# A graph attention kernel: products of half blocks in the first projection too, another order of products, and other first and last graphs

## The chip, the cores and the metric

The kernel runs on one core of one Trainium2 chip. The metric is the device time of one execution in microseconds. TensorE (PE in the profile) multiplies and transposes into eight banks of PSUM; VectorE (DVE) and ScalarE (ACT) do the element-wise work and read the banks; SyncE (SP) issues the DMAs; GpSimd (POOL) has one small power operation per graph. Each engine works through its own queue in order, and semaphores make one wait for another.

## What is computed

Thirty-two graphs of 512 nodes with 512 features go through a normalization, two layers of graph attention and a residual addition. All arithmetic is in float32.

```python
def gat_layer(x, mask, W, a_src, a_dst, bias, concat):
    xl = (x @ W).reshape(B, N, H, F)
    asrc = jnp.einsum('bnhf,hf->bnh', xl, a_src)
    adst = jnp.einsum('bnhf,hf->bnh', xl, a_dst)
    e = jax.nn.leaky_relu(asrc[:, :, None, :] + adst[:, None, :, :], 0.2)
    e = jnp.where(mask[..., None], e, NEG_INF)
    attn = jax.nn.softmax(e, axis=1)
    out = jnp.einsum('bsdh,bshf->bdhf', attn, xl)
    ...
    return out + bias

h = jnp.maximum(_layernorm(x, axis=-1), 0.0)
h = jax.nn.elu(gat_layer(h, mask, W1, att_src1, att_dst1, b1, concat=True))
x = x + gat_layer(h, mask, W2, att_src2, att_dst2, b2, concat=False)
```

The first layer has four heads of 256 features (W1 is 512x1024), the second has one head of 512 (W2 is 1024x512). The mask is the adjacency with its diagonal set.

## The kernel before

Nodes and features lie on 128 partitions in blocks of 128: four node blocks, four blocks of input features, eight of hidden features.

**One graph.** `load` and `load_adj` bring x and the adjacency (two `adj` buffers, so that the third and fourth tile wait until `masks` has used the first two). `norm` is a generator of five steps: statistics, then for each node block the normalized rows and four transposes (`pht`, L187), which ScalarE copies with a Relu into `ht` (one buffer). `masks` makes the 0 / big mask in bfloat16 (three buffers, each used until the second layer of its graph is done, three graphs on); `turned_masks` transposes it (`pm`, L208).

`project1` (L306) multiplies `ht` by W1. For two heads at a time and each node block it makes two results of 128x258 in a PSUM bank, each of four multiplications over the input features; ScalarE copies each into `xl` (L317). The columns 0 and 1 of each head are the score weights, which `weights1` reduces from W1 and the attention vectors, so that the scores come out of the same product. In float32 a multiplication is two instructions of the profile, which is why 64 multiplications show as 128.

`Soft` is the attention. `columns(i)` picks the scores out of `xl`; `rows(i)` transposes them (`pas`, L227), copies them (`ras`, L229) and sends them through DRAM (two DMAs on SP: `das`, L231, and `oas`, L233), so that every partition has the source scores as a row. `first(h)` makes the normalizers of one head: for each node block a Prelu (L263), a masked minimum (L266, VectorE) and an exponential with its sum (L270), then a logarithm and the small rows `r` (L276, L277). `turn(h)` spreads `r` as `rows` does (`prr` on TensorE, `rrr`, `drr`, `orr`). `second(h)` makes the attention weights `p` (L292 on VectorE, L296 on ScalarE, L300 on VectorE).

`gather1` (L325) multiplies `xl` by `p`, two blocks of features per head, eight steps in all, with the elu (ScalarE L339 into `e`, VectorE L340 and L341 into `h1`). `project2` (L371) is the second projection. It is cut into halves of rows, features and columns, and instead of eight products of half blocks it makes seven, of sums of blocks (the Strassen-Winograd form). `sums2` (L355) makes four sums of `h1` on VectorE, `weights2` four sums of W2. A product is four multiplications; three banks per row block m ("a", "g", "b") take the products, and a bank is read between two products that accumulate into it: products 1, 5, 6 and 4 are copied by ScalarE, 2, 7 and 3 are added to `xl2` by VectorE (L404). `gather2` (L429) multiplies the second layer's `p` by `xl2` in four steps, and VectorE adds the residual `xr` (L441), to which `residual_bias` has added the bias (L427); the sum goes out.

**The order.** All is unrolled. Tile's planner orders the instructions of VectorE, ScalarE, GpSimd and SP by its own estimates of when they can run, with the program's order as priority; TensorE's order is written out by hand (`manual_schedule`). Round i of the main loop has three stretches on TensorE: `project1` of graph i + 1; four steps of `gather2` of graph i - 1 and fourteen products of `project2` of graph i; eight steps of `gather1` of graph i + 1. The transposes of other steps are put between them: `late.turn(0)` (second layer of graph i - 1) after the first step of `project1`, `s1.rows(0)` after its fifth of eight; `s1.rows(1)` after the first step of `gather2`, `s1.turn(0)` after the third, the other heads' between the products of `project2`; the second layer's `rows` behind the third step of `gather1`. PSUM has six banks for products (tag "mm") and two for transposes (tag "tp").

Ahead of the loop stand `load`, `weights1`, `norm`, `masks` and `weights2` for graph 0; round -1 has only graph 0's first layer, with all four heads turned before its `gather1`. In the last full round two steps of `gather2` come before and two after `project2`, and the second layer of the last graph follows alone.

## Time and profile before

| | |
|---|---|
| Median of three runs | 3241.77 us (3239.64 to 3250.65) |
| Profiled execution | 3244.41 us, of which the span of its instructions is 3242.4 us |
| Mean granted clock of TensorE | 0.988 |
| DMA read and written | 232.53 MB and 34.54 MB, 82 GB/s over the span |

```profile
## 4 chain that ended last, share of the span: by engine, by line
PE 64%; DMA 13%; DVE 12%; ACT 10%; issue 1%; SPq 0%; POOL 0%; ACTq 0%; DVEq 0%
...
L313 PE MATMUL pxl<-w_sb,ht 128*128 128x258 f32 x4096 | 935.3, 385 | 3.1 <-DVE j L111 3.1
L333 PE MATMUL po<-p,xl 128*128 128x512 f32 x2048 | 890.2, 594 | 0.0
```

The first two lines are the chain of work that ended last, by engine. The others are groups of instructions: line, engine, operation, tiles, shapes and count; then the busy time, the mean length of one in ns, and the idle time ahead of them with what ended it. The mean of one is longer than its share of the busy time, as the multiplications overlap: 935.3 us by 4096 is 0.23 us each. In rows of a timeline the first two columns are start and length in us, and the bracket at the end is the engine's idle time before the row and what ended it. In rows of stretches, after the stretch and its length, stand the busy times with the instructions counted, then the granted clock (1.00 is full speed) and the DMAs' share and GB/s.

### The profile page before, as it was taken

How to read it: one execution, taken by the hardware profiler on the slowest of the kernel's cores; microseconds unless marked ns; L12 is line 12 of the kernel's file. 1: busy time of each engine (PE TensorE's matmuls, PEld its weight loads, DVE VectorE, ACT ScalarE, POOL GpSimd, SP SyncE). 2: the span in 40 equal slices, each digit the busy share in tenths (PEclk: the TensorE clock that was granted, in tenths of full speed). 3: DMA queues.
4: the chain of work that ended last, by engine and by line, in shares of the span. 5: the costliest groups of instructions: out<-in, count | busy, mean ns of one | idle time of the engine just before them, and what ended most of it. 6: DMA issues, size and time to landing. Idle time of an engine off the chain costs nothing.

```text
span 3242.4 us, 35403 instructions
## 1 busy us (share of the span) xinstructions
PE 3142.2 (97%) x12032; PEld 2125.1 (66%) x12032; DVE 2282.4 (70%) x5163; ACT 1785.5 (55%) x3873; POOL 33.2 (1%) x38
## 2 busy tenths in 40 slices
PE   5899999999999999999999999999999999999987
PEld 4576676666676666776666776666766766766754
DVE  7677766677766777766777766777766777766672
ACT  3555655556555556555556555556555555555561
POOL 0000000000000000000000000000000000000000
PEclk8899999999999999999999999999999999999998
DMA  5122222222322122322122322222322222321121
GB/s 185 43 66 82 95 98 76 65 86 81 101 92 82 60 88 84 101 91 76 62 88 88 98 89 80 65 82 95 98 85 72 75 82 95 98 77 60 63 69 49
DMA packets 121462, 269.38 MB, mean 83 GB/s; under 512 B 15552, under 2 KB 22592, under 8 KB 121280
## 3 DMA queue, kind: packets, MB, share of 16 engines
q1 hardware_dynamic: 121280, 267.12, 25.5%
q8 instruction: 94, 1.54, 0.2%
q14 instruction: 88, 0.72, 0.1%
HBM read 232.53 MB, written 34.54 MB: 82 GB/s over the span
## 4 chain that ended last, share of the span: by engine, by line
PE 64%; DMA 13%; DVE 12%; ACT 10%; issue 1%; SPq 0%; POOL 0%; ACTq 0%; DVEq 0%
PE po L333 27%; PE pxl L313 18%; PE po L436 6%; ACT l L270 5%; ACT l L263 5%; DMA oas<-das 4%; PE pxm_1a L381 4%; DVE p L292 4%; DMA orr<-drr 3%; DVE p L300 3%; PE pxm_0a L381 3%; DMA adj<-in_adj_dram 2%; DVE l L266 1%; PE pxm_1b L381 1%; PE pxm_0b L381 1%; DMA das<-ras 1%
## 5 line engine op out<-in xcount | busy, mean ns | idle before, releaser
L313 PE MATMUL pxl<-w_sb,ht 128*128 128x258 f32 x4096 | 935.3, 385 | 3.1 <-DVE j L111 3.1
L333 PE MATMUL po<-p,xl 128*128 128x512 f32 x2048 | 890.2, 594 | 0.0
L313 PEld LDWEIGHTS pxl<-w_sb,ht 128*128 128x128 f32 x4096 | 769.5, 191 | 128.2 <-issue 14.8
L266 DVE CUSTOM_DVE_ANT_0 l<-l,mt 128x512 f32<-128x512 f32 x640 | 426.9, 686 | 546.1 <-ACT l L263 546.1
L333 PEld LDWEIGHTS po<-p,xl 128*128 128x128 f32 x2048 | 387.5, 191 | 473.8 <-issue 456.1
L263 ACT ACTIVATE l<-oas,sc 128x512 f32<-128x512 f32 x640 | 432.7, 709 | 255.0 <-DMA oas<-das 254.0
L296 ACT ACTIVATE p<-p,lo 128x512 f32<-128x512 f32 x640 | 435.9, 717 | 236.0 <-DVE p L292 235.9
L292 DVE SCALAR_TENSOR_TENSOR p<-orr,lo 128x512 f32<-128x512 f32 x640 | 447.6, 745 | 83.0 <-DMA orr<-drr 81.4
L317 ACT ACTIVATE xl<-pxl 128x258 f32<-128x258 f32 x512 | 189.1, 382 | 532.9 <-PE pxl L313 532.1
L436 PE MATMUL po<-xl,p 128*128 128x512 f32 x1024 | 461.9, 597 | 19.8 <-DVE p L300 19.8
L270 ACT ACTIVATE l<-l,low 128x512 f32<-128x512 f32 x640 | 454.1, 710 | 28.5 <-DVE low L266 27.8
L300 DVE TENSOR_TENSOR p<-p,m 128x1024 f32<-128x1024 f32 x320 | 382.6, 1216 | 0.6 <-ACT p L296 0.4
L436 PEld LDWEIGHTS po<-xl,p 128*128 128x128 f32 x1024 | 188.7, 192 | 232.3 <-issue 204.1
L339 ACT ACTIVATE e<-po,b_sb 128x512 f32<-128x512 f32 x256 | 171.0, 679 | 191.0 <-PE po L333 188.0
L381 PE MATMUL pxm_1a<-w_sb,h 128*128 128x257 f32 x768 | 185.9, 384 | 12.2 <-DVE xl L404 10.6
L341 DVE SCALAR_TENSOR_TENSOR h<-po,b_sb,e 128x512 f32<-128x512 f32 x256 | 191.0, 747 | 4.6
L381 PE MATMUL pxm_0a<-w_sb,h 128*128 128x257 f32 x768 | 184.3, 382 | 0.1
L381 PEld LDWEIGHTS pxm_1a<-w_sb,h 128*128 128x128 f32 x768 | 142.5, 189 | 44.4 <-DVE xl L404 20.5
L381 PEld LDWEIGHTS pxm_0a<-w_sb,h 128*128 128x128 f32 x768 | 143.8, 191 | 33.8 <-issue 14.5
L340 DVE TENSOR_SCALAR e<-e 128x512 f32<-128x512 f32 x256 | 107.6, 421 | 77.6 <-ACT e L339 76.5
L381 PE MATMUL pxm_1b<-w_sb,hs 128*128 128x257 f32 x512 | 121.9, 380 | 0.0
L381 PE MATMUL pxm_0b<-w_sb,hs 128*128 128x257 f32 x512 | 121.9, 380 | 0.0
(77 smaller groups left out, 2282.0 us busy)
## 6 DMA issues: line engine op xcount, KB each, us to landing
orr<-drr SPq DMA_DIRECT2D x160, 512.0 KB
x<-in_x_dram SPq DMA_DIRECT2D x128, 256.0 KB
adj<-in_adj_dram SPq DMA_DIRECT2D x128, 256.0 KB
xr<-in_x_dram SPq DMA_DIRECT2D x128, 256.0 KB
oas<-das SPq DMA_DIRECT2D x64, 512.0 KB
out_dram<-xr SPq DMA_DIRECT2D x128, 256.0 KB
oas<-das SPq DMA_DIRECT2D x32, 256.0 KB
w_sb<-in_L_gnn_W_dram SPq DMA_DIRECT2D x8, 512.0 KB
```

Source lines behind the costliest of these rows:

```text
L263: nc.scalar.activation(e, self.asr[i][:, j, :], AF.Prelu, bias=ad[:, d : d + 1], alpha=SLOPE)
L266: nc.vector.tensor_tensor_reduce(out=e, in0=e, in1=MASKT[self.b][:, d, :], scale=-1.0, scalar=BIG, op0=OP.add, op1=OP.min, accum_out=low[: ...
L270: nc.scalar.activation(e, e, AF.Exp, bias=low[:, d : d + 1], scale=-1.0, accum_out=tot[:, d : d + 1])
L292: nc.vector.scalar_tensor_tensor(p[:, u, :], rr[:, 0, :], lo[:, 0, j, u : u + 1], rr[:, 1, :], op0=OP.add, op1=OP.max,)
L296: nc.scalar.activation(p[:, u, :], p[:, u, :], AF.Exp, bias=lo[:, 1, j, u : u + 1])
L300: nc.vector.tensor_tensor(pp, pp, MASK[self.b][:, t : t + 2, :], op=OP.min)
L313: nc.tensor.matmul(ps[:, :W], ht[:, k, t * P : (t + 1) * P], w1_sb[:, k, h, :], start=(k == 0), stop=(k == KT - 1),)
L317: nc.scalar.activation(xl[:, t, h, :], ps[:, :W], AF.Copy)
L333: nc.tensor.matmul(ps, xl[:, s, h, 2 + f * P : 2 + (f + 1) * P], p[:, s, :], start=(s == 0), stop=(s == NT - 1),)
L341: nc.vector.scalar_tensor_tensor(H1[b][:, g, :], ps, bias, e, op0=OP.add, op1=OP.max)
L381: nc.tensor.matmul(ps[:, :W2H], left[n][:, k, m * P : (m + 1) * P], RIGHT[n][:, k, :], start=(first and k == 0), stop=(k == KH - 1), skip_ ...
L436: nc.tensor.matmul(ps, p[:, s, d * P : (d + 1) * P], v[:, s, 1 : DO + 1], start=(s == 0), stop=(s == NT - 1),)
```

## The change

The seven products go into the first projection too, for graphs 1 to 31. `sums` replaces `sums2` for both layers: for the first layer it makes four sums of `ht`, 128x512 each, in the `gather1` before; `w1_sb` holds seven blocks, and `sums_of_weights` makes four of them, for both weights. `project1` becomes 28 products of two multiplications, for four units u (two pairs of heads by two row blocks), in the order FOUR; `project2` takes the order TWO. An entry is (unit, product). Graph 0 keeps plain products in `project1_first`, with its weights in the new layout.

The steps are set anew. In `project1` the turned masks come after products 4, 8, 12 and 16, `late.turn(0)` after 2, `columns(0)` after 20, `rows(0)` after 24, `columns(1)` after 28. The sums of `h1` move from the third step of `project1` behind the first step of `gather2`. `hs` is one buffer for both layers. The tiles `e` and the scratch of the weights' reductions share the tag of `xr`.

For graph 0 the adjacency is loaded ahead of the normalization, the score weights are reduced for heads 0 and 1, the masks follow, then heads 2 and 3; `weights2` and the sums of W1 come after the first projection; two heads are turned ahead of `gather1` and two inside it. In the last rounds the second layer of graph 30 is turned inside the last `gather1`, and `project2` of graph 31 comes ahead of all four steps of `gather2` of graph 30.

```diff
-    w1_sb = const.tile([P, KT, H, W], F32, name="w1_sb")
+    KQ = KT // 2
+    w1_sb = const.tile([P, 7, KQ, H // 2, W], F32, name="w1_sb")
...
+    def halves(w_sb):
+        return {(0, 0): w_sb[:, 0], (0, 1): w_sb[:, 6], (1, 0): w_sb[:, 1], (1, 1): w_sb[:, 2]}
+    def sums_of_weights(w_sb):
+        b11, b21, b22, t4, t1, t2, t3 = (w_sb[:, i] for i in range(7))
+        nc.vector.tensor_sub(t1, t3, b11)
+        nc.vector.tensor_sub(t2, b22, t1)
+        nc.vector.tensor_sub(t3, b22, t3)
+        nc.vector.tensor_sub(t4, b21, t2)
...
+    def scores1(j):
+        at = halves(w1_sb)
+        for c in range(2):
             for a, v in enumerate((as1, ad1)):
+                bc = work.tile([P, FH], F32, tag="l", name=f"a1_{a}_{j}_{c}", bufs=3)
+                nc.sync.dma_start(bc, rows_of(v[2 * j + c], P))
+                for r in range(2):
+                    for k in range(KQ):
+                        junk = work.tile([P, FH], F32, tag="xr", name=f"j1_{a}_{j}_{c}_{r}_{k}", bufs=2)
+                        nc.vector.scalar_tensor_tensor(
+                            junk, at[r, c][:, k, j, 2:], 1.0, bc, op0=OP.mult, op1=OP.mult,
+                            accum_out=at[r, c][:, k, j, a : a + 1],
+                        )
...
-                    junk = work.tile([P, DO], F32, tag="et", name=f"j2_{a}_{r}_{c}_{k}", bufs=2)
+                    junk = work.tile([P, DO], F32, tag="xr", name=f"j2_{a}_{r}_{c}_{k}", bufs=2)
...
+        sums_of_weights(w2_sb)
...
-            sb = work.tile([k, P], F32, tag=f"r{tag}{k}", name=f"r{tag}{name}")
+            sb = work.tile([k, P], F32, tag="spread", name=f"r{tag}{name}")
...
+    def sums(b, a, kh, layer):
+        M = N // 2
+        a11, a12 = a[:, :kh, :M], a[:, kh:, :M]
+        a21, a22 = a[:, :kh, M:], a[:, kh:, M:]
+        hs = work.tile([P, 3, kh, M], F32, tag="hs", name=f"hs{b}_{layer}", bufs=1)
+        s1, s2, s4 = (hs[:, i] for i in range(3))
+        nc.vector.tensor_add(s1, a21, a22)
+        nc.vector.tensor_sub(a21, a11, a21)
+        nc.vector.tensor_sub(s2, s1, a11)
+        nc.vector.tensor_sub(s4, a12, s2)
+        LEFT[b, layer] = {1: a11, 2: a12, 3: s4, 4: a22, 5: s1, 6: s2, 7: a21}
+    def sevens(name, left, w_sb, kh, units, width, order):
+        bank = {}
+        for u, n in order:
+            m, right, to = units[u]
+            acc, first = {1: "a", 2: "g", 5: "b", 6: "a", 7: "a", 3: "b", 4: "a"}[n], n in (1, 2, 5)
+            if first:
+                bank[u, acc] = psum.tile([P, 512], F32, tag="mm", name=f"{name}_{u}{acc}", bufs=6)
+            ps = bank[u, acc][:, :width]
+            for k in range(kh):
+                nc.tensor.matmul(
+                    ps, left[n][:, k, m * P : (m + 1) * P], right(w_sb[:, n - 1], k),
+                    start=(first and k == 0), stop=(k == kh - 1), skip_group_check=True,
+                )
+            if n in (1, 5, 6):
+                nc.scalar.activation(to(*{1: (0, 0), 5: (1, 1), 6: (0, 1)}[n]), ps, AF.Copy)
+            elif n == 4:
+                nc.scalar.activation(to(1, 0), ps, AF.Copy)
+            else:
+                d = to(*{2: (0, 0), 7: (1, 1), 3: (0, 1)}[n])
+                nc.vector.tensor_add(d, ps, d)
+            yield
+    FOUR = (
+        (0, 1), (0, 5), (0, 2), (1, 1), (1, 2), (0, 6), (0, 3), (1, 5), (2, 1), (1, 6), (0, 7), (2, 5),
+        (3, 1), (1, 3), (1, 7), (0, 4), (2, 6), (3, 6), (2, 2), (1, 4), (3, 5), (2, 7), (3, 7), (2, 3),
+        (3, 2), (3, 3), (2, 4), (3, 4),
+    )
+    TWO = (
+        (0, 1), (1, 1), (1, 2), (1, 5), (0, 6), (1, 6), (0, 2), (0, 5), (0, 7), (1, 7), (1, 3), (0, 3),
+        (0, 4), (1, 4),
+    )
...
+    def project1(b):
+        units = [
+            (
+                m,
+                lambda w, k, j=j: w[:, k, j, :],
+                lambda r, c, m=m, j=j: xl[:, 2 * r + m, 2 * j + c, :],
+            )
+            for j in range(H // 2) for m in range(2)
+        ]
+        yield from sevens(f"pxl{b}", LEFT.pop((b, 1)), w1_sb, KQ, units, W, FOUR)
...
-                e = work.tile([P, N], F32, tag="et", name=f"e{b}_{g}", bufs=2)
+                e = work.tile([P, N], F32, tag="xr", name=f"e{b}_{g}", bufs=2)
...
-            (0, 1), (0, 2), (0, 5), (1, 1), (0, 6), (1, 2), (1, 5),
-            (0, 7), (1, 6), (0, 3), (0, 4), (1, 7), (1, 3), (1, 4),
...
     load(0)
     weights1()
+    load_adj(0)
     rest(norm(0))
-    load_adj(0)
+    scores1(0)
     masks(0)
-    weights2()
-    late = None
-    def second_layer(b):
-        return Soft(b, 2, cols2(b), lambda h, p: PS2.__setitem__(b, p))
+    scores1(1)
     with tc.manual_schedule(engines={mybir.EngineType.PE}):
+        load(1)
+        load_adj(1)
+        nm, mt, s1 = norm(1), turned_masks(0), first_layer(0)
+        for n, _ in enumerate(project1_first()):
+            if n >= 4:
+                step(mt)
+            if n == 3:
+                s1.columns(0)
+            if n == 4:
+                s1.rows(0)
+        step(nm)
+        weights2()
+        sums_of_weights(w1_sb)
+        s1.columns(1)
+        step(nm)
+        s1.first(0)
+        s1.rows(1)
+        step(nm)
+        s1.turn(0)
+        s1.first(1)
+        s1.second(0)
+        step(nm)
+        s1.turn(1)
+        s1.first(2)
+        s1.second(1)
+        step(nm)
+        late = None
...
+                if i + 1 < B:
+                    s1 = first_layer(i + 1)
+                    mt = turned_masks(i + 1)
+                    plan = {n: [lambda: step(mt)] for n in (4, 8, 12, 16)}
+                    if late:
+                        plan[2] = [lambda: late.turn(0), lambda: late.second(0)]
+                    if i >= 1:
+                        plan[14] = [lambda: residual_bias(i - 1)]
+                    plan[20] = [lambda: s1.columns(0)]
+                    plan[24] = [lambda: s1.rows(0), lambda: s1.first(0)]
+                    plan[28] = [lambda: s1.columns(1), lambda: s1.first(1)]
+                    for n, _ in enumerate(project1(i + 1), 1):
+                        at_step(plan, n)
+                else:
+                    s1 = None
+                    residual_bias(i - 1)
+                plan = {}
+                if i < B:
+                    plan[1] = [lambda: sums(i, H1.pop(i), KH, 2)]
+                if s1:
+                    for n, f in (
+                        (1, lambda: s1.rows(1)),
+                        (3, lambda: s1.turn(0)), (3, lambda: s1.first(2)),
+                        (4, lambda: s1.second(0)),
+                        (9, lambda: s1.turn(1)), (9, lambda: s1.first(3)),
+                        (10, lambda: s1.second(1)),
+                        (13, lambda: s1.turn(2)),
+                        (14, lambda: s1.second(2)),
+                        (16, lambda: s1.turn(3)),
+                    ):
+                        plan.setdefault(n, []).append(f)
+                if front:
+                    for n in (2, 6, 10, 14):
+                        plan.setdefault(n, []).append(lambda: step(nm))
+                order = [gather2(i - 1) if i >= 1 else iter(())] * 4
+                if last:
+                    at_step(plan, 1)
+                    plan = {
+                        14: [lambda: late.columns(0)],
+                        15: [lambda: late.rows(0), lambda: late.first(0)],
+                        18: [lambda: late.turn(0), lambda: late.second(0)],
+                    }
+                    late = second_layer(i)
+                    order = [project2(i)] * 14 + order
+                elif i < B:
+                    order += [project2(i)] * 14
+                for n, g in enumerate(order, 1):
+                    next(g, None)
+                    at_step(plan, n)
...
             if i + 1 < B:
+                plan = {}
+                if late:
+                    plan[2] = [lambda: late.rows(0), lambda: late.first(0)]
+                if i + 2 == B:
+                    plan[6] = [lambda: late.turn(0)]
+                    plan[7] = [lambda: late.second(0)]
+                if i < 0:
+                    plan[0] = [lambda: s1.turn(2), lambda: s1.first(3), lambda: s1.second(2)]
+                    plan[2] = [lambda: s1.turn(3), lambda: s1.second(3)]
+                else:
+                    plan[1] = [lambda: s1.second(3)]
+                if front:
+                    plan.setdefault(3, []).append(lambda: sums(i + 2, HT.pop(i + 2), KQ, 1))
+                    plan.setdefault(4, []).append(lambda: masks(i + 2))
                 for n, _ in enumerate(gather1(i + 1)):
+                    at_step(plan, n)
```

More of the change, by code (lines that the diff above doesn't have):

```diff
@@ L304, in tile_gat @@
     PS1, PS2, H1, LEFT = {}, {}, {}, {}
-    def project1(b):
-        ht = HT.pop(b)
-        for hp in (0, 2):
+    def sums(b, a, kh, layer):
[9 more added lines that the diff above has]
+        LEFT[b, layer] = {1: a11, 2: a12, 3: s4, 4: a22, 5: s1, 6: s2, 7: a21}
@@ L309, in project1, with project1_first @@
+    FOUR = (
[3 rows of a table added]
+    )
[3 more added lines that the diff above has]
+    )
+    def project1_first():
+        ht = HT.pop(0)
+        at = halves(w1_sb)
+        for j in range(H // 2):
             for t in range(NT):
-                for h in (hp, hp + 1):
-                    ps = psum.tile([P, 512], F32, tag="mm", name=f"pxl{b}_{t}_{h}", bufs=6)
+                for c in range(2):
+                    ps = psum.tile([P, 512], F32, tag="mm", name=f"pxl0_{t}_{j}_{c}", bufs=6)
@@ L520, in tile_gat @@
[L520 to L531 removed]
+            last = i == B - 1
```

179 lines of the change are left out of this document (41 added, 138 removed).

## The prediction

> **What bounds the kernel now.** I read the page's busy shares first, then the busy times by stretch, then TensorE's waits, then single stretches in order of time.
>
> ```profile
> PE 3142.2 (97%) x12032; PEld 2125.1 (66%) x12032; DVE 2282.4 (70%) x5163; ACT 1785.5 (55%) x3873; POOL 33.2 (1%) x38
> ```
> ```profile
> core 0: us, PE busy (x) PEld busy (x) DVE busy (x) ACT busy (x) POOL busy (x), PEclk, DMA share, GB/s
> 0.00:125.40 125.40, 76.28 (x246) 49.56 (x247) 92.17 (x293) 48.75 (x100) 3.96 (x9) 0.82 0.42 137
> ...
> 3150.90:3242.40 91.50, 57.77 (x180) 35.10 (x178) 30.57 (x52) 14.89 (x30) 0.00 (x0) 0.82 0.14 49
> ```
> ```profile
> 2779.00:2877.00 98.00, 98.00 (x381) 66.76 (x380) 70.40 (x157) 56.11 (x122) 1.01 (x1) 1.00 0.27 86
> ```
> ```profile
> PE prr L227 <- DVE r L277: 29.4, 6, 10.1
> PE po L436 <- DVE p L300: 19.8, 2, 10.6
> PE pxm_1a L381 <- DVE xl L404: 10.6, 19, 0.8
> ...
> PE pxm_1a L381 <- ACT xl L399: 1.2, 2, 0.9
> ```
>
> TensorE is the bound: a whole graph (2779 to 2877) is 98 us of it without a gap and at full clock, while VectorE (DVE) has 70. It loses time in two places only: 49 us of the first 125 (to the end of the first graph's `gather1`) and 34 us of the last 91.5 (from the end of the last `gather1`). Between them the waits on evictions in `project2` are the only ones that recur, 11.8 us in all. So work taken from TensorE is worth its whole time, until something that stood beside it is late.
>
> **The change part by part.** *Fewer products.* These are consecutive pieces of one graph; columns are start, length, line, instructions.
>
> ```profile
> 1504.91 0.27 PE L227 MATMUL pas<-identf,sc 128*8 128x128 f32 x1
> 1505.02 10.61 PE L313 MATMUL pxl<-w_sb,ht 128*128 128x258 f32 x48
> 1515.46 3.60 PE L436 MATMUL po<-xl,p 128*128 128x512 f32 x8
> ...
> 1526.32 0.27 PE L227 MATMUL prr<-identf,r 128*8 128x128 f32 x1
> ...
> 1529.87 1.90 PE L381 MATMUL pxm_0a<-w_sb,h 128*128 128x257 f32 x8
> 1531.61 1.90 PE L381 MATMUL pxm_0g<-w_sb,h 128*128 128x257 f32 x8
> ```
>
> From start to start, 48 instructions take 10.44 us, 0.2175 each. `project1` has 64 multiplications of two instructions, 128; after it has 28 products of two multiplications, 112. That `project2` pays 1.74 us for 8 (again 0.2175), with a new bank each time, says that shorter groups cost nothing more. 16 x 0.2175 = 3.48 us, for 31 graphs (the first keeps the plain form): **-107.9 us**.
>
> *More work on VectorE.* Of 28 evictions, 12 become adds out of PSUM (16 copies stay on ScalarE, as before), and four sums of 128x512 are new.
>
> ```profile
> L441 DVE TENSOR_TENSOR xr<-po,xr 128x512 f32<-128x512 f32 x128 | 87.2, 681 | 31.3 <-PE po L436 31.3
> ...
> L363 DVE TENSOR_TENSOR hs<-h 128x1024 f32<-128x1024 f32 x32 | 39.2, 1224 | 1.1
> ...
> L404 DVE TENSOR_TENSOR xl<-pxm_1b,xl 128x257 f32<-128x257 f32 x32 | 13.4, 418 | 3.7 <-PE pxm_1b L381 3.7
> ```
>
> 12 x 0.42 = 5.0 us, and the sums lie between half of L363 (0.61) and L441 (0.68): 2.6 us. VectorE goes from 71.3 (2282.4 / 32) to 79 us in a graph of some 95: still not the bound on average. What matters is its order, since each engine takes its queue in turn. In FOUR a bank is written again five products after its last one, so an eviction has four products, 3.48 us, to be done. Three things stand in that queue during `project1`:
>
> ```profile
> 1506.07 0.43 DVE L196 TENSOR_SCALAR m<-adj 128x512 bf16<-128x512 int32 x1 [3.17 <-DMA adj<-in_adj_dram]
> ...
> 1553.75 0.40 DVE L404 TENSOR_TENSOR xl<-pxm_0b,xl 128x257 f32<-128x257 f32 x1
> ...
> 1594.77 2.74 DVE L292 SCALAR_TENSOR_TENSOR p<-orr,lo 128x512 f32<-128x512 f32 x4 [1.60 <-DMA orr<-drr]
> 1597.43 2.35 DVE L300 TENSOR_TENSOR p<-p,m 128x1024 f32<-128x1024 f32 x2
> ```
>
> `late.second(0)` holds VectorE for 5.0 us from L292 on, plus 1.6 us of waiting for `orr`; the mask waits 3.2 us for its `adj` DMA; and in `project2` an add (1553.75) came some 5 us after its product. The four big sums (4 x 1.22) leave `project1` for `gather2`, which makes room for the adds. Four banks per graph (7 to 4) hang on it. Bounds: nothing (all evictions inside 3.48 us) to 1.5 us per graph (the 5 us add, once); I take 0.6, nearer to the waits of `project2` (11.8 / 31 = 0.4): **+18 us**. Nothing is gained here beyond the old waits.
>
> *TWO* leaves at least three products (5.2 us) between a bank's products where one (1.7) stood before the last of row block 1: the 11.8 us go, **-11**.
>
> *The first score rows.* `columns(0)` waits for all of heads 0 and 1, which FOUR ends with product 20 of 28; `rows(0)` follows product 24. Four products (3.48) and not 48 instructions (10.44) now stand between the transpose `pas` and `gather2`; `turn(0)`'s `prr` stays behind the third of `gather2`. In the rows above `prr` is 21.41 us behind `pas`; after, 21.41 - 6.96 = 14.45. What has to happen in between (copy, two DMAs on SP, `first(0)`) ends with L277:
>
> ```profile
> 1407.74 0.27 PE L227 MATMUL pas<-identf,sc 128*8 128x128 f32 x1
> ...
> 2976.81 0.27 PE L227 MATMUL pas<-identf,sc 128*8 128x128 f32 x1
> ```
> ```profile
> 1423.27 0.15 DVE L277 SCALAR_TENSOR_TENSOR r<-sc,low 128x4 f32<-128x4 f32 x1
> ...
> 1521.36 0.15 DVE L277 SCALAR_TENSOR_TENSOR r<-sc,low 128x4 f32<-128x4 f32 x1
> ...
> 2990.91 0.15 DVE L277 SCALAR_TENSOR_TENSOR r<-sc,low 128x4 f32<-128x4 f32 x1
> ```
>
> That is 15.7 us (1407.74), 16.6 (1504.91, the longest) and 14.25 (2976.81, without `adj` transfers beside it). The cover is gone: against 14.45 it is late by -0.2 to 2.15 us. After, masks and `adj` loads follow `late.second(0)`, which starts two products earlier, so they should be over when the later `pas` comes; the four sums of `h1` now want VectorE in the same stretch, but it was idle 6 us there. I take 0.8 us for 30 graphs: **+24** (0 to 65).
>
> *Graph 1* has no `gather2` before it, so `prr` follows `pas` by four products, `pas(1)` and a block of `pht`, 4.1 us.
>
> ```profile
> 143.94 0.27 PE L227 MATMUL pas<-identf,sc 128*8 128x128 f32 x1
> 158.25 0.27 PE L227 MATMUL prr<-identf,r 128*8 128x128 f32 x1 [1.97 <-DVE r L277]
> 158.35 3.44 PE L381 MATMUL pxm_0a<-w_sb,h 128*128 128x257 f32 x8
> ```
>
> It takes 14.3, so TensorE stands 10.2 us where it stood 2.0; the slow products behind (3.44 for 1.74) are slow already: **+8** (6 to 10).
>
> *First graph.*
>
> ```profile
> 14.35 0.43 DVE L111 SCALAR_TENSOR_TENSOR j<-w_sb,a 128x256 f32<-128x256 f32 x1 [3.67 <-DMA a<-in_L_gnn_att_src_dram]
> ...
> 110.99 2.35 DVE L300 TENSOR_TENSOR p<-p,m 128x1024 f32<-128x1024 f32 x2
> ```
> ```profile
> 57.73 0.27 PE L227 MATMUL pas<-identf,sc 128*8 128x128 f32 x1
> ...
> 73.19 0.27 PE L227 MATMUL prr<-identf,r 128*8 128x128 f32 x1 [1.97 <-DVE r L277]
> ...
> 95.28 30.30 PE L333 MATMUL po<-p,xl 128*128 128x512 f32 x64
> ```
>
> Rows of VectorE, then of TensorE. x and `w1`, 3 MB, are there at 14.35. The second weight's 32 reductions and its sums stood between the masks of graph 0; now they come after `project1_first`, whose products run nearly unbroken: the reductions for heads 0 and 1 end near 23, four row blocks (7 x 1.74 more) near 35, and `pas`, one block later, comes at an estimated 38. `gather1` starts when two heads are ready, not four. But `weights2` (32 of at most 0.42, as L404) and both `sums_of_weights` (eight like L363, four of them new) stand ahead of `first(0)` in the program, and their data, 4.75 MB more at the rate of the first 3, land at about 38. VectorE is then taken until about 60; four heads at 8 us (5.0 for L292 and L300, 3 for L266 at L441's 0.68) and some 11 us of `norm` and `gather1` (16 such operations) follow: the last head at 103, where L300 for it ended at 113; two products more make 110 against 125.4. **-15** (-5 to -25).
>
> *Last graph.*
>
> ```profile
> 3150.77 0.27 PE L227 MATMUL prr<-identf,r 128*8 128x128 f32 x1
> 3161.65 9.19 PE L436 MATMUL po<-xl,p 128*128 128x512 f32 x16 [10.61 <-DVE p L300]
> ...
> 3198.47 0.27 PE L227 MATMUL pas<-identf,sc 128*4 128x128 f32 x1
> ...
> 3212.25 0.38 PE L227 MATMUL prr<-identf,r 128*8 128x128 f32 x1 [10.06 <-DVE r L277]
> 3221.77 16.72 PE L436 MATMUL po<-xl,p 128*128 128x512 f32 x32 [9.15 <-DVE p L300]
> ```
>
> `late.turn/second` of graph 30 move into the last `gather1`, so the 10.6 us go (less 1 us at the earlier `prr`). `project2` (24.4 us) comes first, `pas` after one of four blocks of `gather2` (27.8), and r 13.7 later, of which 10.4 are covered by the other three blocks where 3.4 were. 41.5 + 9.5 + 16.7 + 3.9 = 71.6 for 91.5: **-20** (-14 to -22).
>
> *At nothing:* the eight weight DMAs for four (same bytes), and `e` sharing a tag with `xr`. The latter makes the residual's loads wait on SP for the last `e` of `gather1`, with `drr` queued behind them; that delays `late.second(0)` by 2 us at most, and that ends 14 us before `gather2` needs it (1599.8 against 1515.5 + 98).
>
> **Sum:** -107.9 + 18 - 11 + 24 + 8 - 15 - 20 = -103.9. The profiled execution (3242.4 us of span, 3244.4 in all) becomes 3140.5; against the median of 3241.8, 2.6 lower, **3138**.
>
> **The rivals.** (a) *All is covered*: r takes 14.25 and the evictions fit. Then 42 us of waits are not paid: 3096. For it: the idle VectorE and the adj transfers that have moved ahead. (b) *r is late every time*, at 2.2 us as in the longest row, with 0.9 us at the adds: 3138 + 30 x 1.4 + 31 x 0.3 = 3189. For it: contention is the rule in the rows above. (c) *The other side: the four sums get in front of `first(0)`.* They are released when `project1` ends, about when `oas` lands; put ahead of L266 they take 4.9 us, and r is late by 15.7 + 4.9 - 14.45 = 6.1. The gap before the last `gather2` (9.15 us) made 32 instructions take 16.72 us and not 4 x 3.44, so 3.0 us more per gap for the clock. 30 x (6.1 - 0.8 + 3.0) = 249: 3387. It decides from 4.3 us of wait per graph ((103.9 + 24) / 30). Against it: 6 us of idle time lie exactly there. The Trainium skill ("TensorE: Matmul & The Clock Gate", What's actually happening) says that TensorE's clock falls to half after an idle window of about 3.4 us; by that the clock would be lost from 3.4 us of wait on, earlier than (c) decides, and a wait of 3.5 us with 3.0 lost would give 3138 + 30 x 5.7 = 3309. The rows agree as far as they go: 9 us lost the clock, 0.8 us did not, and the 0.8 us of the forecast is safe. (d) *The adds eat it*: 3.4 us per graph of bank waits leave no change; it needs every graph's four 7-to-4 pairs late by 0.85 us.
>
> **How the numbers follow.** The forecast has 0.50 (alone 3112 to 3165), (a) 0.23, (b) 0.18, (c) 0.05, (d) 0.04. The range takes the forecast, (a) and (b) with their ends: 3092 to 3192; outside are (c), (d) and the tails. A measurement here tells about 0.3%, 10 us, from no change. Faster 0.92, same 0.03, slower 0.05.
>
> **What would show it.** 3472 instructions in `project1` beside 128 for graph 0, where there were 4096; a graph of about 95.5 us; waits of `prr` on L277 near 1 us once per graph and some 10 us in graph 1; waits of `project1` on the adds below 1 us per graph; `gather1` of graph 0 ending near 110; 72 us behind the last `gather1`. Wrong it would be if `prr` waits over 3 us, if DVE's order puts the adds behind `late.second(0)` for more than 3.5 us, or if the first graph waits for weights.

## The result and the profile after

The changed kernel takes 3147.86 us (median of four runs, 3145.24 to 3151.34) where the kernel before took 3243.13 beside it: a ratio of 0.9704, 95% interval 0.9684 to 0.9724. The forecast was 3138, in a range of 3092 to 3192. The profiled execution took 3145.24 us, 3143.5 of it the span; the sum had 3140.5 for it.

The page's busy time by engine, of after:

```profile
PE 3036.8 (97%) x11536; PEld 2027.3 (64%) x11536; DVE 2494.4 (79%) x5663; ACT 1806.2 (57%) x3873; POOL 44.0 (1%) x38
```

TensorE has 496 instructions less, 16 for each of 31 graphs, and is still the bound; VectorE has gone from 70 to 79% of the span. The same stretches were then cut in both traces: to the end of the first `gather1`, graph 1, 29 whole rounds, the last round to the end of the last `gather1`, and the rest. First before's (its first and last row stand in the prediction), then after's; each row has the stretch, its length, the busy time of PE with its instructions, those of the other engines, and the granted clock.

```profile
125.40:214.20 88.80, 85.64 (x344) 61.17 (x343) 58.86 (x139) 52.99 (x117) 1.01 (x1) 0.98 0.17 51
214.20:3055.30 2841.10, 2826.89 (x10905) 1914.81 (x10904) 2036.49 (x4540) 1615.04 (x3509) 28.20 (x28) 1.00 0.26 83
3055.30:3150.90 95.60, 95.60 (x362) 64.49 (x360) 64.35 (x139) 53.82 (x117) 0.00 (x0) 1.00 0.18 64
```
```profile
0.00:112.50 112.50, 73.24 (x247) 47.10 (x247) 95.12 (x299) 48.99 (x100) 4.73 (x9) 0.88 0.45 143
112.50:206.10 93.60, 81.74 (x329) 57.92 (x328) 65.87 (x155) 53.70 (x117) 1.37 (x1) 0.95 0.15 49
206.10:2966.40 2760.30, 2730.04 (x10442) 1824.79 (x10441) 2233.01 (x5004) 1634.93 (x3509) 37.93 (x28) 1.00 0.26 86
2966.40:3064.90 98.50, 94.37 (x347) 61.92 (x346) 68.49 (x152) 54.00 (x117) 0.00 (x0) 0.98 0.20 69
3064.90:3143.50 78.60, 57.37 (x179) 35.55 (x177) 31.92 (x53) 14.61 (x30) 0.00 (x0) 0.87 0.17 62
```

The length of a stretch less PE's busy time is what PE stood still. In the 29 rounds PE works 96.9 us less, but stands 30.3 us where it stood 14.2: 80.8 us gained. The table sets the prediction's terms beside it, spread over the same stretches (a round: -3.48 products, +0.6 adds, -0.36 old waits, +0.8 r).

| Stretch | predicted | measured |
|---|---|---|
| first graph | -15 | -12.9 |
| graph 1 | +5 | +4.8 |
| 29 rounds | -71 | -80.8 |
| last round and what follows | -22.5 | -10.0 |
| span | -103.9 | -98.9 |

TensorE's waits of after (what waits, for what, us in total, times, longest), for the whole span and then for the 29 rounds alone:

```profile
PE prr L245 <- DVE r L295: 40.2, 32, 8.5
PE pxl_0a L348 <- DVE xl L359: 19.5, 30, 1.5
```
```profile
PE pxl_0a L348 <- DVE xl L359: 18.8, 29, 1.5
PE prr L245 <- DVE r L295: 11.3, 27, 0.7
```

Once per graph a product waits for an add (0.65 us), and nearly once for r (0.4). The waits of `project2` that recurred before (10.6 and 1.2 us) are gone. The wait for the add is always the same pair. In order of time, VectorE's rows and then TensorE's:

```profile
1547.86 2.74 DVE L310 SCALAR_TENSOR_TENSOR p<-orr,lo 128x512 f32<-128x512 f32 x4 [1.39 <-DMA orr<-drr]
1550.51 2.35 DVE L318 TENSOR_TENSOR p<-p,m 128x1024 f32<-128x1024 f32 x2
1552.78 0.42 DVE L359 TENSOR_TENSOR xl<-pxl_0a,xl 128x258 f32<-128x258 f32 x1
```
```profile
1547.64 1.03 PE L348 MATMUL pxl_0a<-w_sb,ht 128*128 128x258 f32 x4
...
1553.26 1.14 PE L348 MATMUL pxl_0a<-w_sb,ht 128*128 128x258 f32 x4 [0.82 <-DVE xl L359]
```

Product (0,7) starts at 1547.64. Its add stands in VectorE's queue behind all of `late.second(0)` (L310, L318) and is done at 1553.2; four products later TensorE wants the bank for (0,4) and waits 0.82 us.

### The profile page after: what moved, and what is told of

Read it like the earlier page. It is cut to its first block, busy times and chain, and to the rows that moved or that the text cites. A ratio compares the mean times of both kernels' runs of the same rounds, so it can differ in the third digit from the quotient of the medians.

```text
span 3143.5 us, 35412 instructions
## 1 busy us (share of the span) xinstructions
PE 3036.8 (97%) x11536; PEld 2027.3 (64%) x11536; DVE 2494.4 (79%) x5663; ACT 1806.2 (57%) x3873; POOL 44.0 (1%) x38
## 4 chain that ended last, share of the span: by engine, by line
PE 78%; DVE 9%; DMA 9%; ACT 1%; SPq 1%; issue 1%; POOL 0%; DVEq 0%; ACTq 0%; POOLq 0%
PE po L414 27%; PE po L477 10%; PE pxm_0a L348 7%; PE pxm_1a L348 7%; DMA orr<-drr 4%; PE pxm_1b L348 3%; PE pxm_0b L348 3%; DVE p L310 3%; PE pxl_2a L348 3%; DVE p L318 3%; PE pxl_3a L348 3%; DMA drr<-rrr 2%; DMA x<-in_x_dram 2%; PE pxl_0a L348 2%; PE pxm_0g L348 2%; PE pxl_3b L348 2%
## 5 line engine op out<-in xcount | busy, mean ns | idle before, releaser
L314 ACT ACTIVATE p<-p,lo 128x512 f32<-128x512 f32 x640 | 442.4, 719 | 254.2 <-DVE p L310 253.1
L284 DVE CUSTOM_DVE_ANT_0 l<-l,mt 128x512 f32<-128x512 f32 x640 | 415.8, 685 | 130.6 <-ACT l L281 129.5
L310 DVE SCALAR_TENSOR_TENSOR p<-orr,lo 128x512 f32<-128x512 f32 x640 | 448.4, 747 | 77.9 <-DMA orr<-drr 77.7
L318 DVE TENSOR_TENSOR p<-p,m 128x1024 f32<-128x1024 f32 x320 | 384.2, 1218 | 0.0
L482 DVE TENSOR_TENSOR xr<-po,xr 128x512 f32<-128x512 f32 x128 | 87.3, 682 | 43.0 <-PE po L477 42.9
L288 ACT ACTIVATION_READ_ACCUMULATOR l<-l,low 128x1 f32 x640 | 120.2, 188 | 0.0
L348 PE MATMUL pxl_0a<-w_sb,ht 128*128 128x258 f32 x372 | 99.2, 389 | 19.5 <-DVE xl L359 19.5
```

Of the source, the lines that this page charges most:

```text
L284: nc.vector.tensor_tensor_reduce(out=e, in0=e, in1=MASKT[self.b][:, d, :], scale=-1.0, scalar=BIG, op0=OP.add, op1=OP.min, accum_out=low[: ...
L288: nc.scalar.activation(e, e, AF.Exp, bias=low[:, d : d + 1], scale=-1.0, accum_out=tot[:, d : d + 1])
L310: nc.vector.scalar_tensor_tensor(p[:, u, :], rr[:, 0, :], lo[:, 0, j, u : u + 1], rr[:, 1, :], op0=OP.add, op1=OP.max,)
L314: nc.scalar.activation(p[:, u, :], p[:, u, :], AF.Exp, bias=lo[:, 1, j, u : u + 1])
L318: nc.vector.tensor_tensor(pp, pp, MASK[self.b][:, t : t + 2, :], op=OP.min)
L348: nc.tensor.matmul(ps, left[n][:, k, m * P : (m + 1) * P], right(w_sb[:, n - 1], k), start=(first and k == 0), stop=(k == kh - 1), skip_gr ...
```

## The experiments

Eleven kernels ran. Ratios are to the kernel before, run beside it on the same chip, which takes the difference between chips out (its medians were 3244.0 to 3250.1 us).

| Kernel | median us | ratio, 95% interval | 29 rounds, us |
|---|---|---|---|
| plain first projection | 3212.32 | 0.9883 (0.9868 to 0.9898) | 2830.2 |
| old order of project2 | 3148.91 | 0.9691 (0.9675 to 0.9707) | 2761.9 |
| short FOUR | 3277.31 | 1.0081 (1.0057 to 1.0104) | 2886.6 |
| turn(0) a step later | 3147.16 | 0.9684 (0.9670 to 0.9699) | 2762.7 |
| after again | 3150.24 | 0.9696 (0.9683 to 0.9709) | 2762.2 |
| sums first in the last round | 3142.87 | 0.9676 (0.9663 to 0.9688) | 2761.3 |
| sums behind first(0) | 3230.85 | 0.9940 (0.9919 to 0.9961) | 2841.6 |
| (0,4) two products later | 3120.78 | 0.9607 (0.9594 to 0.9619) | 2733.8 |
| three edits | 3094.09 | 0.9536 (0.9521 to 0.9552) | 2719.1 |
| four edits | 3101.41 | 0.9557 (0.9541 to 0.9572) | 2717.7 |
| before with the shared tag | 3228.30 | 0.9951 (0.9938 to 0.9964) | 2824.0 |

### Plain products in the first projection

```diff
-                    for n, _ in enumerate(project1(i + 1), 1):
+                    for n, _ in enumerate(project1_first(i + 1), 1):
...
-                    plan.setdefault(3, []).append(lambda: sums(i + 2, HT.pop(i + 2), KQ, 1))
```

> The changed kernel with plain products in the first projection of every graph, steps set as before the change; both ends, TWO and the new layout stay. If the gain comes from TensorE's instructions: 31 x 3.48 = 108 us come back, less the waits that only the products cause (19.5 us at the adds, 11 to 20 us at the transposes of the rows): 70 to 90 us slower than the changed kernel, 3217 to 3238. If the gain is that of the two ends and of the bank spacing, and the products only pay for their adds: within 30 us of the changed kernel, 3150 to 3178.

The 29 rounds get 69.9 us longer, and the whole is 1.8% (58 us) slower than after by the ratios, 66 by the spans, a little under the 70 to 90 that were expected. The products' 100.9 us are therefore worth some 70 here, as the adds and the late r come with them. What this kernel keeps of the change (the two ends, the shared tag, TWO, the sums of `h1` in `gather2`) gives the other 1.2%.

### The old order in project2

```diff
     TWO = (
-        (0, 1), (1, 1), (1, 2), (1, 5), (0, 6), (1, 6), (0, 2), (0, 5), (0, 7), (1, 7), (1, 3), (0, 3),
-        (0, 4), (1, 4),
+        (0, 1), (0, 2), (0, 5), (1, 1), (0, 6), (1, 2), (1, 5), (0, 7), (1, 6), (0, 3), (0, 4), (1, 7),
+        (1, 3), (1, 4),
```

> The changed kernel with the old order of project2's fourteen products. If the spacing of the banks is what took the old waits away: the 10 to 12 us of waits on adds come back, up to 25 as VectorE is fuller now, so 3157 to 3173. If the waits went because VectorE's load moved out of that stretch: within 4 us of the changed kernel.

No difference, and the waits on the adds of `project2` do not come back: no `pxm_1a` is among the waits. So TWO is not needed to be rid of them. (Whether TWO alone would have done it in the kernel before, no run shows.)

### The shared tag alone, in the kernel before

What else had changed for VectorE during `project2`? In the trace of before the two halves of `residual_bias` (L427, 1.2 us each) run there: the residual's buffers have no other user, so the planner can pull them ahead. After, the buffers share a tag with `e` of `gather1`, and `residual_bias` runs only behind that.

```diff
-                e = work.tile([P, N], F32, tag="et", name=f"e{b}_{g}", bufs=2)
+                e = work.tile([P, N], F32, tag="xr", name=f"e{b}_{g}", bufs=2)
```

> The kernel before with one edit: e shares its tag with xr, as after. The old order of project2's products is kept, as are the old first projection and all places. Theory A (the 11.8 us of waits in project2 went because residual_bias, 2.4 us on VectorE, cannot run during project2 any more once xr has to wait for e's buffers, and not because of TWO): L427 runs in project1, the waits of pxm_1a fall from 10.6 us to below 3, and the time falls by about 10 us, ratio 0.997. Theory B (they went because the sums of h1 or the score chain moved): the waits stay near 10 us, ratio 1.000 or more.

VectorE's rows of before, then of this kernel (the second half follows 2.6 us later); then its row of waits:

```profile
1531.91 1.23 DVE L427 TENSOR_TENSOR xr<-xr,b_sb 128x1024 f32<-128x1024 f32 x1
...
1544.65 1.18 DVE L427 TENSOR_TENSOR xr<-xr,b_sb 128x1024 f32<-128x1024 f32 x1
```
```profile
1487.81 1.21 DVE L427 TENSOR_TENSOR xr<-xr,b_sb 128x1024 f32<-128x1024 f32 x1
```
```profile
PE pxm_1a L381 <- DVE xl L404: 2.2, 6, 0.6
```

In before the rows lie inside `project2` (1529.87 to 1557.4 on TensorE); here inside `project1` (1481.57 to about 1511). In all 29 rounds it is the same. The `pxm_1a` waits fall from 10.6 to 2.2 us, the 29 rounds by 17.1 and the whole by 0.5%. One word in one line, an edit that was counted at nothing, does by itself what was credited to the new order. That it acts through the place of `residual_bias` is read from these rows; no run moved L427 alone.

### FOUR with few products between

```diff
     FOUR = (
-        (0, 1), (0, 5), (0, 2), (1, 1), (1, 2), (0, 6), (0, 3), (1, 5), (2, 1), (1, 6), (0, 7), (2, 5),
-        (3, 1), (1, 3), (1, 7), (0, 4), (2, 6), (3, 6), (2, 2), (1, 4), (3, 5), (2, 7), (3, 7), (2, 3),
-        (3, 2), (3, 3), (2, 4), (3, 4),
+        (0, 1), (0, 2), (0, 5), (1, 1), (0, 6), (1, 2), (1, 5), (0, 7), (1, 6), (0, 3), (0, 4), (1, 7),
+        (1, 3), (1, 4), (2, 1), (2, 2), (2, 5), (3, 1), (2, 6), (3, 2), (3, 5), (2, 7), (3, 6), (2, 3),
+        (2, 4), (3, 7), (3, 3), (3, 4),
```

> The changed kernel with the first projection's 28 products in the old order of project2, twice: one or two products (0.87 to 1.74 us) between a bank's product and its next in place of four (3.48 us). If evictions behind other work on VectorE need 2 to 5 us, the four pairs 7 to 4 wait 0.5 to 1.5 us each and others some: 60 to 180 us slower than the changed kernel, and the waits stand on the adds. If evictions are in time anyway: under 20 us slower.

Slower than before by 0.8%. The row of its waits, and of its 29 rounds:

```profile
PE pxl_1a L348 <- DVE xl L359: 84.0, 30, 3.8
```
```profile
208.60:3095.20 2886.60, 2785.03 (x10441) 1854.13 (x10440) 2221.87 (x5004) 1636.03 (x3509) 37.92 (x28) 0.98 0.25 82
```

Waits of 2.8 us per graph, and beside them 55 us more of busy time for the same instructions than after (2785.03 for 2730.04), at a mean clock of 0.98: the waits are long enough to slow what follows them. Only one of the four pairs waits, (1,7) to (1,4). The distance between two products on one bank is worth 126 us in the rounds, more than the products themselves. Rival (d) of the prediction is thereby real as a mechanism, at 4.4 us per graph; FOUR avoids most of it.

### turn(0) a step later

```diff
-                        (3, lambda: s1.turn(0)), (3, lambda: s1.first(2)),
-                        (4, lambda: s1.second(0)),
+                        (4, lambda: s1.turn(0)), (3, lambda: s1.first(2)),
+                        (5, lambda: s1.second(0)),
```

> The changed kernel with the transposes of head 0's rows (turn(0)) behind the fourth step of gather2 instead of the third, 3.4 us later. If r is late by 0.4 us per graph as the waits say: these 11 us go and nothing comes in their place, since p of head 0 has 20 us until gather1: 3134 to 3140, and the transposes wait only in graph 1. If the later spread delays p of head 0: waits of gather1 on L318 appear and the time stays within 4 us or grows.

Same time. Of the waits for r only five are left, all at the two ends; but the waits at the add of (0,7) grow from 19.5 to 36.6 us:

```profile
PE pxl_0a L348 <- DVE xl L359: 36.6, 30, 2.3
PE prr L245 <- DVE r L295: 27.2, 5, 8.5
```

The 11 us had only changed their place. As long as the add of (0,7) is late, any time that TensorE gains ahead of it is given back there.

### After once more

> The changed kernel itself once more, on the chip of the three runs beside it, so that they have something to be compared with. Ratio to before 0.970 as in the first measurement; sums of waits like those of the trace after (pxl_0a 19.5 us, prr 40.2).

It gave 0.9696 and 2762.2 us for the 29 rounds (2760.3 in the first trace). The waits at the add are 24.0 us in this trace, 21.3 of them in the rounds, and those for r 40.9: some us of scatter between two executions. The next three kernels ran beside it.

### The sums of h1 behind first(0)

Rival (c) put the four sums ahead of `first(0)` on VectorE. In small, that is what happened; the rows of after show TensorE's `pas` and VectorE's next rows:

```profile
1465.70 0.27 PE L245 MATMUL pas<-identf,sc 128*8 128x128 f32 x1
```
```profile
1471.86 1.22 DVE L334 TENSOR_TENSOR hs<-h,hs 128x1024 f32<-128x1024 f32 x1
1472.99 0.69 DVE L284 CUSTOM_DVE_ANT_0 l<-l,mt 128x512 f32<-128x512 f32 x1
```

The last sum ends where the first minimum of `first(0)` starts, 7.29 us behind `pas`. The edit queues the sums of `h1` behind the last L284 of `first(0)`:

```diff
+    def sums_after(mark, i, h1):
+        with tc.issue_after(getattr(mark, "ins", mark)):
+            sums(i, h1, KH, 2)
...
                     plan[1] = [lambda: sums(i, H1.pop(i), KH, 2)]
+                    if s1:
+                        plan[1] = [lambda: sums_after(s1.mark0, i, H1.pop(i))]
```

> The four sums of h1 may be scheduled on VectorE only behind the last instruction of first(0). Theory A (the wait of prr in the rounds, 0.4 us per graph, comes from the sums that stand ahead of first(0), 0.7 us of L284): pas to r falls from about 15 to 14.3 us, the prr waits of the rounds fall from 11.3 us to near 0, and the time falls by at most 11 us if nothing else gets late. Theory B (VectorE has to end the same work ahead of project2, so that the wait only changes its place, as when turn(0) was moved a step later): pxl_0a or pxm waits grow by as much, time the same within 0.2%.

Rows of this kernel: `pas` and `prr` of `turn(0)` on TensorE, then the first minimum on VectorE, then TensorE's waits in the rounds.

```profile
1497.55 0.27 PE L245 MATMUL pas<-identf,sc 128*8 128x128 f32 x1
...
1512.01 0.27 PE L245 MATMUL prr<-identf,r 128*8 128x128 f32 x1
```
```profile
1503.84 0.69 DVE L284 CUSTOM_DVE_ANT_0 l<-l,mt 128x512 f32<-128x512 f32 x1 [1.62 <-ACT l L281]
```
```profile
PE pxl_0a L352 <- DVE xl L363: 67.6, 29, 3.2
PE prr L245 <- DVE r L295: 12.5, 17, 1.6
```

The minimum starts 6.29 us behind `pas`, 1.0 sooner. Over the rounds r of head 0 is ready 13.70 us behind `pas` (median) where it was 14.96, and `prr` of `turn(0)` stands at 14.46 without a wait, in every round. So the first half of theory A holds: the sums are why r was late. And yet the kernel is 2.5% slower than after: the waits at the same add go from 18.8 to 67.6 us, again with loss of clock (busy time 2761.3 for 2730.0). The 12.5 us at `prr` are those of another step: all 17 stand at `late.turn(0)`, in `project1`. The rows show where that lateness begins. First after, then this kernel: `pas` of the second layer, on TensorE, and its copy `ras`, on VectorE.

```profile
1520.99 0.27 PE L245 MATMUL pas<-identf,sc 128*4 128x128 f32 x1
```
```profile
1525.26 0.27 DVE L247 COPY ras<-pas 4x128 f32<-4x128 f32 x1
```
```profile
1551.86 0.27 PE L245 MATMUL pas<-identf,sc 128*4 128x128 f32 x1
```
```profile
1558.44 0.27 DVE L247 COPY ras<-pas 4x128 f32<-4x128 f32 x1
```

With the sums later, the copy stands in VectorE's queue behind the whole p of the first layer's last head (1552.53 to 1557.78), in after behind a part of it: 6.8 us behind `pas` in the median of the rounds, for 3.6. The second layer's r comes 19.4 us behind `pas` for 15.3, `late.second(0)` starts 2.2 us later (28.9 for 26.7), and the add of (0,7) stands behind it. That is theory B, the wait in another place, far stronger than expected.

### (0,4) two products later

```diff
-        (3, 1), (1, 3), (1, 7), (0, 4), (2, 6), (3, 6), (2, 2), (1, 4), (3, 5), (2, 7), (3, 7), (2, 3),
+        (3, 1), (1, 3), (1, 7), (2, 6), (3, 6), (0, 4), (2, 2), (1, 4), (3, 5), (2, 7), (3, 7), (2, 3),
```

> In FOUR the product (0,4) comes two places later, so six products and not four lie between the add of (0,7) and it. Theory A (the 0.65 us per graph on the adds is this one pair, whose add stands behind late.second(0)): pxl_0a's waits fall from 19.5 us to below 3, and the time falls by about 19 us plus the slower first product behind a wait (0.1 x 30), 0.6%. Theory B (second(0) holds the adds of another unit as long): the same sum of waits appears at pxl_1a or pxl_2a, same time.

The wait on the add in after once more, in the 29 rounds:

```profile
PE pxl_0a L348 <- DVE xl L359: 21.3, 29, 2.6
```

Here no wait on an add of `project1` is left, and nothing took its place (`prr` waits 42.2 us for 40.9). Against after on the same chip it is 29.5 us faster (3120.78 for 3150.24), more than the 19 and some 3 expected: the 29 rounds lose 28.4 us, 0.98 per graph, where the trace of after beside it shows 0.73 of waiting. The rest is read from the rows of after: products start 0.87 us apart but take 1.03, so a wait, which is counted from the end of the product ahead, costs 0.16 more; and the product behind it takes 1.14 and not 1.03 (1553.26 and 1547.64). Together that is 0.27, and 0.98 less 0.73 is 0.25.

### The last round

TensorE's rows behind the last `gather1` of after, and VectorE's:

```profile
3059.62 0.33 PE L245 MATMUL prr<-identf,r 128*8 128x128 f32 x1 [3.43 <-DVE r L295]
3059.75 5.28 PE L414 MATMUL po<-p,xl 128*128 128x512 f32 x8
...
3075.25 3.79 PE L348 MATMUL pxm_1b<-w_sb,hs 128*128 128x257 f32 x8 [5.00 <-DVE hs L331]
```
```profile
3069.43 2.35 DVE L318 TENSOR_TENSOR p<-p,m 128x1024 f32<-128x1024 f32 x2
3071.70 2.35 DVE L468 TENSOR_TENSOR xr<-xr,b_sb 128x1024 f32<-128x1024 f32 x2
3073.97 1.22 DVE L331 TENSOR_TENSOR hs<-h 128x1024 f32<-128x1024 f32 x1
```

`project2` comes first there and needs the sums; but `second(0)` of graph 30 and `residual_bias`, wanted only by `gather2` after 24 us of products, stand ahead of them. The edit emits them behind the sums:

```diff
-                    residual_bias(i - 1)
+                    if not last:
+                        residual_bias(i - 1)
...
                     at_step(plan, 1)
+                    late.second(0)
+                    residual_bias(i - 1)
...
-                    plan[7] = [lambda: late.second(0)]
```

> In the last round VectorE gets the four sums of graph 31's h1 ahead of second(0) of graph 30 and of the residual's bias; TensorE's order is as in after. Theory A (the -20 of the last graph came out at -6.5 because these two steps, 7 us, stand ahead of the sums): the wait of 5.0 us of pxm_1b goes to 0-1 us and the products behind run at full speed (16 instructions 3.5 us and not 6.4); the sums push second(0) later, but that is needed only by gather2, 24 us on; span 7-8 us shorter. Theory B (project2's start is set by L281 and the copies at the end of gather1, not by these steps): the wait stays at 4-5 us, same time.

```profile
3070.58 1.90 PE L348 MATMUL pxm_1b<-w_sb,hs 128*128 128x257 f32 x8
3073.38 1.98 PE L348 MATMUL pxm_0a<-w_sb,hs 128*128 128x257 f32 x8 [0.90 <-DVE hs L333]
```

The wait of 5.0 us becomes one of 0.9, and the products run at full speed. From the end of the last `gather1` it is 71.5 us (3065.4 to the span's end, 3136.9), 7.1 less than after. The medians differ by 7.4 us, at the edge of what the intervals tell apart; the rows settle it.

### Three edits together, and a fourth

> The changed kernel with three edits at once: (0,4) two products later, the sums of h1 first in the last round, and turn(0) one step of project2 later. The first two alone gave ratios 0.9607 and 0.9676 for 0.9696. Theory A (the place where the waits went when turn(0) alone moved, the add of (0,7), has room now): the prr waits of the rounds (11 us) go and nothing takes their place, so 0.9607 - 0.0020 - 0.0035 = 0.955. Theory B (second(0) of the first layer, then a step later, pushes VectorE's work on to another bank): the 11 us come back elsewhere, 0.9585.

```profile
205.40:2924.50 2719.10, 2718.34 (x10441) 1828.68 (x10440) 2207.46 (x5007) 1622.80 (x3509) 35.81 (x28) 1.00 0.26 87
```

TensorE stands 0.8 us in 29 rounds, where it stood 30.3. The same later `turn(0)` that brought nothing alone is worth 14.7 us (2733.8 to 2719.1) once the add is out of the way. Against plain products (2830.2) the new ones are now worth 111.1 us in the rounds, not 69.9. At 0.9536 this is the fastest version, 4.6% below before.

The fourth edit turns head 0 of graph 1 only behind five products of `project2`, and heads 1 and 2 two and one steps later.

```diff
-                        (4, lambda: s1.turn(0)), (3, lambda: s1.first(2)),
-                        (5, lambda: s1.second(0)),
-                        (9, lambda: s1.turn(1)), (9, lambda: s1.first(3)),
+                        (4 if i else 9, lambda: s1.turn(0)), (3, lambda: s1.first(2)),
+                        (5 if i else 10, lambda: s1.second(0)),
+                        (9 if i else 11, lambda: s1.turn(1)), (9, lambda: s1.first(3)),
...
```

> As the three edits, and in graph 1, where no gather2 stands between pas and prr, turn(0) comes behind five products of project2 and turn(1) and turn(2) two and one steps later. If the 8.5 us of prr in graph 1, and the slow clock behind them, were the whole +4.8 us of that graph: graph 1 goes from 93.6 to about 83, 8 to 10 us less than the three edits. If the later turns make gather1(1) wait for its last heads: 0 to 5 us less, with po waits on p in its place.

It is 7.3 us slower than the three, where 0 to 10 less were expected: graph 1 takes 98.8 us for 92.0. Its row of waits, and ScalarE's row that ends the wait:

```profile
PE pxm_0a L348 <- ACT xl L354: 9.5, 1, 9.5
```
```profile
159.60 0.37 ACT L354 ACTIVATE xl<-pxm_0a 128x257 f32<-128x257 f32 x1
```

From 143.6 to 159.6 ScalarE works through `first` of all four heads; the copy out of product (0,1), made by 144.8, comes only then, and product (0,6) waits for its bank. TensorE waits for ScalarE's whole queue instead of for r.

## Why the prediction came out near

**What bounds it** was right: TensorE at full clock in the rounds, and every instruction taken from it counts. 463 instructions fewer in 29 rounds lowered its busy time by 96.9 us (464 x 0.2175 is 100.9). A wait adds busy time too (the overlap of two products, and the slower one behind it), and after has more waits: with the same instructions the three edits, almost without waits, are busy 2718.3 us and not 2730.0. (The `project2` waits were not quite the only ones to recur before: seven of `prr` on the copies of `ht`, 2.2 us, did too.)

**The adds** (+18): the mechanism was right, to the pair of the four and the step in front of it; the size was too small. The waits are 0.65 to 0.73 per graph against 0.6, but their cost is 0.98, with the lost overlap and the slower product behind. In 31 graphs that is 30 us. A sign that the prediction named for being wrong did come: the add of (0,7) is done 4.5 us behind its product (1548.67 to 1553.20), more than 3.5. It costs only the part beyond the four products between. Rival (d) has a slip: 3.4 us of waits would come on top of the 0.6 in the sum, so no change needs about 4.

**r late** (+24 at 0.8 us for 30 graphs): right in kind, 0.4 us of waiting and 0.51 of cost (14.7 / 29). The prediction took the sums of `h1` to fit into VectorE's idle time; they cost 1.3 us of the way from `pas` to r (14.96 for 13.70), and without them r is in time for 14.45. Rival (c) is what happened in kind, with 1.3 us in place of 4.9: the sums start at 1468.10, 2.4 us behind `pas`, when VectorE has nothing of `first(0)` to do yet.

**TWO** (-11) was the wrong step with nearly the right sum, which is luck. The waits went, but the old order doesn't bring them back, and the shared tag takes most of them away from the kernel before. That is worth 17.1 us in 29 rounds, not 10: 10.9 less of standing and 6.2 less of busy time for the same work. The part headed "at nothing" held this edit and reasoned about its DMAs on SP only; that it also forbids the planner to pull `residual_bias` forward was overlooked.

These three explain why the rounds gained 80.8 us and not 71: r cost 8 us less and the old waits were worth 7 more, while the adds cost 11 more. Of the remaining 5 or 6, some 3 are waits that the shared tag left in the kernel before (TensorE still stands 3.3 us in its rounds) and after doesn't have, and 1.9 are the scatter of after's two traces.

**The first graph** (-15) measured -12.9 and **graph 1** (+8) 8.3 (4.8 and the 3.48 of its products), within their bounds; the nine other kernels with the same first part ended it at 112.6 to 115.3, so 2 us are within its scatter. The marks on the way came as forecast too: `pas` at 38.8 for 38, the last head's p at 105.0 for 103.

**The last graph** (-20) is the step that failed most: last round and rest together gave -10.0 for -22.5. Two things were missed. The sums of graph 31's `h1` were taken to be ready when `project2` starts; they stood behind `second(0)` and `residual_bias`, and with these moved the end takes 71.5 us, where the prediction had 71.6. And the earlier `prr` in the last `gather1` was given 1 us in words, which 71.6 for 91.5 leaves out; it waits 3.43, and the eight products behind it take 5.28 instead of 3.60: 5.1 in all. 7.1 and 5.1 of the missing 12.5 are these.

So the total was nearer than its terms, by luck: a shortfall of 12.5 us at the end and a gain of 9.8 in the rounds offset each other.

## What to carry to other kernels

Where a bank (or any buffer) is read between two writes, look in the trace for the longest run of work that stands ahead of the reading engine's instruction, and put that much of the writer's other work between: one pair that is two products too early gave away 28 us beside a gain of 95 here. A wait that goes when its own cause is moved may only have gone to the next tight place, so remove the tightest first and try the others again behind it. And a change of a buffer's tag is a change of order: ask what the planner can no longer pull forward.

## What the runs showed of the hardware

**Short waits cost more than they last, and the clock goes earlier than expected.** The kernels with long waits at the adds give waits of all lengths ahead of the same work. Rows of the sums behind `first(0)`, then of the short FOUR, then stretches of the short FOUR, where the figure behind the five busy times is the granted clock:

```profile
608.53 1.14 PE L352 MATMUL pxl_0a<-w_sb,ht 128*128 128x258 f32 x4 [1.98 <-DVE xl L363]
```
```profile
2866.45 1.78 PE L352 MATMUL pxl_0a<-w_sb,ht 128*128 128x258 f32 x4 [2.04 <-DVE xl L363]
```
```profile
1316.12 1.14 PE L348 MATMUL pxl_1a<-w_sb,ht 128*128 128x258 f32 x4 [2.37 <-DVE xl L359]
```
```profile
1615.88 2.09 PE L348 MATMUL pxl_1a<-w_sb,ht 128*128 128x258 f32 x4 [2.44 <-DVE xl L359]
```
```profile
1316.10:1318.80 2.70, 2.68 (x12) 2.29 (x13) 1.72 (x7) 0.77 (x2) 0.00 (x0) 1.00 0.20 28
...
1615.80:1618.80 3.00, 2.92 (x7) 2.35 (x8) 1.70 (x8) 0.39 (x1) 0.00 (x0) 0.50 0.30 81
```

Up to 1.98 us no wait at these adds cost any clock. Between 2.04 and 2.72 some did and some did not: a wait of 2.37 us left it at 1.00, one of 2.44 in the same kernel, at the same product, halved it for some 3 us. Above 2.72 us all did. The Trainium skill ("TensorE: Matmul & The Clock Gate", What's actually happening) says that the clock halves after an idle window of about 3.4 us, and that the windows run freely, not counted from the kernel's start. The halving agrees with it, and windows that run freely would give such a scatter, which no run here tests; the length does not agree: here 2.04 us were enough. Nor does one wait stand alone: in the kernel before, graph 1's `prr` waits 1.97 us (158.25), soon after a wait of 0.92, and there the clock is 0.55 for the next 3.5 us. The prediction's bound for the clock, 3.4 us, was too far out; its conclusion for waits of 0.8 us holds.
